# Layer 0's mixture of experts: the residual in SBUF, two zeroed tables of sums, and the fold of layer 1's weights among the expert blocks

## The chip, the core and the metric

The kernel runs on one core of a Trainium2 chip. The metric is device time in microseconds (us) of one execution. Engines are named as the profile names them: PE is TensorE (matmul), PEld its weight load, DVE VectorE, ACT ScalarE, POOL GpSimd, SP SyncE. SP, ACT and POOL can also issue DMA transfers; the indirect ones (gather and scatter by a list of rows) are issued by POOL.

## What is computed

Four layers, each a gated cross-attention and a gated feed-forward, act on x of 4 x 256 tokens with 256 features. The change is in the feed-forward of layer 0, a mixture of 16 experts (hidden width 176) of which every token takes 6, beside one shared expert (hidden width 352):

```python
x = x + tanh(g_ffn[0]) * L0_ffn(layernorm(x), ...)

def L0_ffn(x, ...):
    probs = softmax(x @ gate_w.T)
    _, idx = top_k(probs + gate_b, 6)
    cw = probs at idx, 0 elsewhere                       # (T, 16)
    y = sum over e of cw[:, e] * ((silu(x @ W1[e].T + B1[e]) * (x @ W3[e].T + B3[e])) @ W2[e].T + B2[e])
    z = (silu(x @ ws1.T + bs1) * (x @ ws3.T + bs3)) @ ws2.T + bs2
    return y + z
```

Layer 1's attention needs products of its own weight matrices only (`Wq`, `w_kc_q`, `W_qr`, `W_kr`, `w_kc_kv`, `Wo`), with no token in them. The kernel folds them ahead, inside layer 0's mixture; this is called the fold.

## The kernel before

The program is written with a layer that inserts all waits and that orders each engine's instructions ahead of time by the program's order and an estimate of when operands are ready; so instructions can stand in another order on an engine than in the code. The 1024 tokens are 8 tiles of 128 (`x[t]`, views of one SBUF tensor `stream`). Tiles with one tag share a fixed number of buffers: `xn` six, `t4` six, the weight slots `C` three (`C_SLOTS`), PSUM `mm` four and `wide` two.

**Weights through the slots.** `loads` (L234 to L241) is a list of weight loads in order of use: layer 0's, then layer 1's fold (`L1_qr`, `L1_kv`, `L1_qk0/1`, `L1_wq0/1`, `L1_wo0/1`), layer 1's feed-forward (`L1_w1`, `L1_w2`), then layers 2 and 3. `used(name)` (L253) frees a slot and issues the next load on SP, each as one DMA of up to 1 MB (`whole`, L207).

**`ffn0` (L1391), the mixture.** It normalises x, stores the normal rows to DRAM (`xd`), and makes a generator `routing()` that goes step by step through `chosen` (softmax, top 6) and `placed` (L1061: which tokens fall into which block of 128 rows). The last six steps of `placed` make, for each of the 6 choices and each of the 8 token tiles, two float16 one-hots on VectorE: `h` (L1132, 128x128) and `v` (L1133, 128x63), whose product on TensorE (L1137) adds up the row numbers. L1148 to L1150 make the lists `scatter` and `gather` from them.

Beside the routing runs the shared expert in 14 units: `up(g, f)` (matmuls at L424, Silu L1431, product L1432) and `down(t)` (L1441), whose result `gated_add` (L458) multiplies by the gate and adds to `x[t]`, in one VectorE instruction that reads PSUM. After each unit comes one routing step, and from the third unit on one step of the fold (`fold1`, L783: matmuls at L794, L812, L825 and, in `fold_output`, L581; eleven steps with work). While a fold step is made, `busy` sends its copies from PSUM to ScalarE (`evacuate`, L136).

Then `keep_rows` (L371) writes x to the DRAM table `sums0[0]`. The second table `sums0[1]` was zeroed during layer 0's attention (L353). The class `Experts` (L1180) works through the blocks. 55 blocks (`SURE0`) are always used; those beyond stand under an `If` on the number of blocks, which comes first in the program (L1351). `blocks` (L1358) goes over i:

- `fetch(i + 4)`: POOL gathers 128 rows of `xd` (L1206) into one of the `xn` buffers
- `turn(i)`: two PE transposes (L1218), a DVE copy (L1219), the tokens' weight (L1230), and a load of the expert's offset into a PE register (L1240) from `near`, which DVE copies for eight blocks at once at every eighth block (L1223)
- `turn_hidden(i - 2)`: transposes of the hidden rows (L1280), an ACT copy (L1282)
- `up(i - 1)`: the bias (L1249), the products (L1253), Silu on ACT (L1272), the product on DVE (L1273)
- `down(i - 2)`: products (L1290), a copy into `ring` by DVE or ACT (L1299, L1301), and POOL's scatter that adds the rows to one of the two DRAM tables in turn (L1305)
- `between(i)`: whatever is left of the fold, which is nothing by then.

The last three blocks (`HOT0`) are not scattered. Their results stay in SBUF, DVE makes one-hots `hits` for them (L1323) during the loop, and `add` (L1331) multiplies them on PE (L1339) and adds them to x (L1341). Before that, `collect` (L1477) loads table 0 over x, table 1 into `more`, and adds the two (L1488). Layer 1's attention begins with a layer norm (L382 to L397) and transposes (L409).

Of the kernel before, what the change touches and what calls it, by code (L numbers as in the profile page):

```python
# [30 lines left out]
F32 = mybir.dt.float32  # L31
# [8 lines left out]
P = 128  # L40
# [42 lines left out]
C_SLOTS = 3  # L83
FIXED = 2 * DC + 8 + 2 * E0 + E0 + 8 + 2 * E3 + 4 + NB0 + 8 + 2 * NT + 1 + L + 1 + 2 * len(HS0)
# [4 lines left out]
def tile_flamingo(ctx: ExitStack, tc: tile.TileContext, a: dict, out: bass.AP):  # L89
# [116 lines left out]

    def whole(src, parts=P):  # L207
        def load(w):
            nc.sync.dma_start(out=w[:parts, : src.shape[1]], in_=src)

        return load

    def halves(src, n):
        def load(w):
            nc.sync.dma_start(
                out=w[:, : n * src.shape[1]].rearrange("p (c f) -> p c f", c=n),
                in_=src.rearrange("(c p) f -> p c f", p=P),
            )

        return load  # L220

    def head_attention(layer, quant):
        def load(w):
            nc.sync.dma_start(out=w[:, :1024], in_=a[f"L{layer}_q_out"])
            nc.sync.dma_start(out=w[:DC, 1024:1536], in_=a[f"L{layer}_kv"])
            if quant:
                nc.sync.dma_start(
                    out=w[:, 1536:2048].rearrange("p (c d) -> p c d", c=2),
                    in_=a["L2_weight"].rearrange("(c p) d -> p c d", p=P),
                )  # L230

        return load

    loads = [(f"L0_qk{i}", whole(a["L0_qk"][i])) for i in range(NQ)]  # L234
# [10 lines left out]
    def issue(upto=C_SLOTS):  # L245
        while at[0] < len(loads) and at[0] - at[1] < upto:
            name, load = loads[at[0]]
            w = sb.tile([P, 2048], F32, tag="C", name=f"w_{name}", bufs=C_SLOTS)
            load(w)
            loaded[name] = w  # L250
            at[0] += 1

# [53 lines left out]
    def prepare():  # L306
# [46 lines left out]
        for half in range(2):  # L353
            zeroed(sums0[1][half * TH : (half + 1) * TH], zeros)
# [248 lines left out]
    def streamed(name, cols, n):  # L603

        return [
            lambda i=i: (loaded[f"{name}{i}"][:, :cols], n, lambda: used(f"{name}{i}")) for i in range(2)
        ]
# [175 lines left out]
    def fold1():  # L783


        w_qr = loaded["L1_qr"][:CQH].rearrange("q (s h r) -> q s h r", s=2, h=NH)
        inner = t4([P, NP, DK], "inner")
        for h8 in range(2):
            w_kcT = loaded[f"L1_qk{h8}"][:CQH].rearrange("q (h s k) -> q h s k", h=NP, s=2)
# [16 lines left out]
        w_kr = loaded["L1_kv"][:, NH * DC : NH * DC + NP * DC].rearrange("r (i d) -> r i d", i=NP)  # L806
# [13 lines left out]
        for h8 in range(2):  # L820
            w_q = loaded[f"L1_wq{h8}"].rearrange("k (h d) -> k h d", h=NP)
# [569 lines left out]
    def ffn0(gate):  # L1391
# [17 lines left out]
        def folded():  # L1409
            if ended:  # L1410
                return
# [491 lines left out]
```

## Time and profile before

| | |
|---|---|
| median of 3 runs | 934.46 us (933.23 to 937.22) |
| the profiled execution | 937.0 us, its span 934.9 us |
| granted TensorE clock, mean | 0.963 of full speed |
| PE busy | 850.5 us, 91% of the span |
| DVE, ACT, POOL busy | 515.8, 286.1, 317.9 us |
| shared expert and routing | from about 222 us to 272 us of the span |
| first gather, last gather, last scatter issued at | 268.35, 432.88, 448.20 us |
| last expert matmul of the loop ends | 443.9 us |
| first transpose of layer 1's attention | 463.93 us |

A line of a view in order of time has: start, duration, engine, line of the kernel, operation, out<-in with shapes, how many, and in brackets the idle time of that engine before it with what ended it. A line of the costliest groups has: line, engine, operation, out<-in, shapes, count, then busy time in us and the mean of one in ns, then idle time before it and what ended most of that. Busy time of POOL's indirect DMAs is the time to make the transfer's descriptors, not the transfer.

### The profile page before, as it was taken

The page shows a single profiled execution, that of the slowest core. Times are in us where ns is not written, and L with a number is a line of the kernel's source. Part 1 is how long each engine was busy: PE and PEld are TensorE (multiplying, and loading weights), DVE is VectorE, ACT ScalarE, POOL GpSimd, SP SyncE. Part 2 cuts the span into 40 slices and gives each one's busy share as a digit, 9 for nine tenths or more (in the row PEclk, how much of TensorE's full clock was granted, in tenths as well). Part 3 has the DMA queues.
Part 4 walks back from the last instruction along what each step waited for, and adds up shares of the span by engine and source line. Part 5 has one row for each costly group of instructions (what it writes and reads, how often), then busy time and mean ns, then how long its engine had stood idle before and what let it go on. Part 6 is the DMA issues. An engine that isn't in the chain of part 4 may idle for free.

```text
span 934.9 us, 12575 instructions
## 1 busy us (share of the span) xinstructions
PE 850.5 (91%) x4395; PEld 544.5 (58%) x4395; DVE 515.8 (55%) x1319; ACT 286.1 (31%) x545; POOL 317.9 (34%) x248
## 2 busy tenths in 40 slices
PE   5999998999978999899599978999889899999993
PEld 3544335875746777576446864755555556566662
DVE  3667446755843435333466787968767864222220
ACT  1221103434212332223133428526535531122220
POOL 0445442320027888887102220003202402244321
PEclk8999999999989999999899999989889999999997
DMA  9410218101684554555740000450000012122222
GB/s 343 139 35 6 96 48 270 48 23 28 215 248 82 87 87 80 85 83 80 219 159 1 1 1 1 143 200 1 1 23 1 1 47 64 46 47 46 35 23 63
DMA packets 38481, 74.90 MB, mean 80 GB/s; under 512 B 6225, under 2 KB 26290, under 8 KB 37042
## 3 DMA queue, kind: packets, MB, share of 16 engines
q1 hardware_dynamic: 24050, 53.34, 16.7%
q0 software_dynamic: 14016, 19.94, 13.4%
q8 instruction: 39, 0.64, 0.3%
q10 hardware_dynamic: 352, 0.79, 0.2%
q14 instruction: 24, 0.20, 0.1%
HBM read 58.87 MB, written 16.22 MB: 80 GB/s over the span
## 4 chain that ended last, share of the span: by engine, by line
PE 74%; DVE 9%; DMA 8%; ACT 4%; issue 2%; POOL 2%; SPq 0%; another core or an unknown queue 0%; POOLq 0%; ACTq 0%; DVEq 0%
PE wide L424 14%; PE wide L1264 8%; PE mm L1290 7%; PE wide L1253 6%; PE mm L424 5%; PE mm L659 4%; DMA xs<-xd,big 2%; PE wide L644 2%; PE mm L1665 2%; PE mm L454 2%; PE mm L1649 2%; PE mm L1280 2%; DMA sums<-ring,big 2%; PE wide L944 2%; PE mm L709 2%
## 5 line engine op out<-in xcount | busy, mean ns | idle before, releaser
L440 POOL TENSOR_TENSOR attn<-attn,sm 128x1024 f32<-128x1024 f32 x32 | 60.8, 1901 | 281.9 <-DVE sm L439 228.5
L1273 DVE SCALAR_TENSOR_TENSOR blk<-wide,blk 128x176 f32<-128x176 f32 (+1 forms) x75 | 37.0, 494 | 148.0 <-ACT blk L1272 141.0
L424 PE MATMUL wide<-xT,big 128*128 128x512 f32 (+1 forms) x240 | 111.3, 611 | 0.3 <-ACT xT L140 0.2
L1305 POOL DMA_INDIRECT sums<-ring,big x52 | 82.7, 1590 | 18.7 <-issue 7.8
L686 DVE TENSOR_TENSOR rope<-wide,big 128x512 f32<-128x512 f32 x96 | 59.6, 684 | 50.1 <-PE wide L424 50.1
L1253 PE MATMUL wide<-big,blk 128*128 x220 | 79.2, 478 | 3.3 <-issue 1.6
L1206 POOL DMA_INDIRECT xs<-xd,big x55 | 56.1, 1019 | 67.0 <-PE mm L581 43.1
L424 PEld LDWEIGHTS wide<-xT,big 128*128 128x128 f32 (+1 forms) x240 | 44.1, 192 | 57.1 <-issue 49.8
L1264 PE MATMUL wide<-big,blk 128*128 x160 | 74.3, 606 | 2.6 <-DMA sums<-x 2.2
L1272 ACT ACTIVATE blk<-wide 128x176 f32<-128x176 f32 (+1 forms) x75 | 29.4, 392 | 137.5 <-PE wide L1264 69.0
L1290 PE MATMUL mm<-big,blk 88*128 x220 | 58.2, 385 | 2.8 <-ACT blk L1282 2.1
L659 PE MATMUL mm<-vo,attnT 128*128 128x256 f32 x256 | 58.6, 382 | 1.5 <-ACT attnT L455 1.5
L1290 PEld LDWEIGHTS mm<-big,blk 88*128 88x128 f32 x220 | 42.0, 193 | 19.4 <-ACT blk L1282 3.8
L659 PEld LDWEIGHTS mm<-vo,attnT 128*128 128x128 f32 x256 | 47.4, 190 | 9.0 <-ACT attnT L455 3.2
L1253 PEld LDWEIGHTS wide<-big,blk 128*128 128x128 f32 x220 | 40.6, 197 | 18.6 <-issue 6.1
L455 ACT COPY attnT<-mm 128x512 f32<-128x512 f32 x64 | 34.6, 588 | 53.6 <-PE mm L454 53.2
L1264 PEld LDWEIGHTS wide<-big,blk 128*128 128x128 f32 x160 | 29.3, 194 | 33.3 <-issue 33.3
L438 DVE TENSOR_REDUCE sm<-attn 128x16 f32<-128x1024 f32 x32 | 38.9, 1215 | 16.2 <-ACT attn L432 13.7
L1305 POOL DMA_INDIRECT sums<-ring,scratch x20 | 31.5, 1573 | 41.0 <-ACT ring L1301 17.0
L1206 POOL DMA_INDIRECT xs<-xd,scratch x20 | 19.4, 972 | 73.5 <-PE mm L1218 49.7
L1219 DVE COPY blk<-mm 128x256 f32<-128x256 f32 x75 | 31.4, 419 | 17.0 <-PE mm L1218 14.4
L454 PE MATMUL mm<-ident,attn 128*128 128x128 f32 x256 | 35.1, 282 | 6.2 <-POOL attn L440 6.1
(311 smaller groups left out, 1607.2 us busy)
## 6 DMA issues: line engine op xcount, KB each, us to landing
big<-in_L_w_gate_up SPq DMA_DIRECT2D x8, 1024.0 KB, 8.9
big<-in_L_w SPq DMA_DIRECT2D x3, 1408.0 KB, 8.1
big<-in_L_w_down SPq DMA_DIRECT2D x8, 512.0 KB, 6.1
w_L_qk<-in_L_qk SPq DMA_DIRECT2D x4, 896.0 KB
big<-in_L_w SPq DMA_DIRECT2D x3, 768.0 KB, 7.1
big<-in_L_wo SPq DMA_DIRECT2D x1, 2048.0 KB, 13.0
xd<-xn SPq DMA_DIRECT2D x16, 128.0 KB, 1.8
w_L_wq<-in_L_wq SPq DMA_DIRECT2D x2, 1024.0 KB, 4.8
```

The costliest lines, as they stand in the source:

```text
L424: nc.tensor.matmul(ps, w(c), xT[:, c, :], start=(c == 0), stop=(c == 1))
L438: nc.vector.tensor_reduce(sm, e, AX.X, ALU.add)
L440: nc.gpsimd.tensor_tensor(e, e, sm.unsqueeze(2).to_broadcast([P, groups, n]), ALU.mult)
L454: nc.tensor.transpose(ps[:, i * P : (i + 1) * P], ev[:, pr * P : (pr + 1) * P], ident)
L659: nc.tensor.matmul(ps[:, :D], aT[:, s, :], vo[:, s, :], start=(s == 0), stop=(s == NP - 1))
L686: nc.vector.tensor_tensor(m[:, s, :].rearrange("q (b t) -> q b t", t=S), ps[:, s, :].rearrange("q (b t) -> q b t", t=S), table, ALU.mult,)
L1206: nc.gpsimd.indirect_dma_start(out=xs, out_offset=None, in_=self.xd, in_offset=bass.IndirectOffsetOnAxis(ap=self.gather[:, b : b + 1].bitc ...
L1253: nc.tensor.matmul(ps[:, 0, : 2 * n], st[:, c * P : (c + 1) * P], self.w[:, bass.ds(r + c * 2 * n, 2 * n)], start=False, stop=(c == 1),)
L1264: nc.tensor.matmul(ps[:, k, :n], st[:, c * P : (c + 1) * P], self.w[:, bass.ds(r + (2 * c + k) * n, n)], start=(c == 0), stop=(c == 1),)
L1273: self.weighted = nc.vector.scalar_tensor_tensor(s, lin, self.weight.pop(b), s, ALU.mult, ALU.mult)
L1290: nc.tensor.matmul(ps[:, :D], hT[:k, j * P : (j + 1) * P], self.w[:k, bass.ds(r + j * D, D)], start=(j == 0), stop=(j == self.n - 1),)
L1305: nc.gpsimd.indirect_dma_start(out=self.sums[b % len(self.sums)], out_offset=bass.IndirectOffsetOnAxis(ap=self.scatter[:, b : b + 1].bitca ...
```

## The change

Six things in one diff; the computed result is the same.

1. x stays in SBUF. `keep_rows` is not called for layer 0; both tables are zeroed during layer 0's attention. `collect` loads both tables into four `t4` tiles, table 0 on SP and table 1 on ACT, and returns `last`, which adds the two tables to x on DVE (eight adds where there were four), after the held blocks' `add`.
2. The fold is no longer stepped in the shared expert's units but in `between(i)`, at i = 5, 9, ..., 49: eleven steps with work, a twelfth that ends it. Its copies alternate between ACT and DVE.
3. During the loop (`paced`) weight loads are cut in pieces of 512 columns; one piece is issued after each block, and `ready(name)` issues what is still missing of a tile before its use.
4. The shared expert's result is multiplied by the gate on ACT into an `xn` tile, and added to `x[t]` on POOL.
5. The one-hots `v` of token tiles 3 to 7 are made on POOL (30 of 48).
6. `near` is copied four blocks before its first use, except for block 0.

```diff
     def whole(src, parts=P):
-        def load(w):
-            nc.sync.dma_start(out=w[:parts, : src.shape[1]], in_=src)
-        return load
+        def pieces(w):
+            n = src.shape[1]
+            step = PIECE if paced[0] else n
+            return [move(w[:parts, i : min(i + step, n)], src[:, i : min(i + step, n)]) for i in range(0, n, step)]
+        return pieces
...
     def issue(upto=C_SLOTS):
         while at[0] < len(loads) and at[0] - at[1] < upto:
-            name, load = loads[at[0]]
+            name, pieces = loads[at[0]]
             w = sb.tile([P, 2048], F32, tag="C", name=f"w_{name}", bufs=C_SLOTS)
-            load(w)
+            waiting.extend((name, piece) for piece in pieces(w))
             loaded[name] = w
             at[0] += 1
+        if not paced[0]:
+            forward(len(waiting))
+
+    def forward(n):
+        for _ in range(min(n, len(waiting))):
+            waiting.pop(0)[1]()
+
+    def ready(name):
+        while any(name == of for of, _ in waiting):
+            forward(1)
+        return loaded[name]
...
-        for half in range(2):
-            zeroed(sums0[1][half * TH : (half + 1) * TH], zeros)
+        for sums in sums0:
+            for half in range(2):
+                zeroed(sums[half * TH : (half + 1) * TH], zeros)
...
-                nc.vector.tensor_scalar(
+                engine = nc.vector if t < alone else nc.gpsimd
+                engine.tensor_scalar(
                     v[:, t, :], block16[:, :nb], blk[:, m : m + 1], number[:, t : t + 1], ALU.is_equal, ALU.mult
                 )
...
-            if b < self.sure and b % 8 == 0:
-                n = min(8, self.sure - b)
-                self.near = small([1, 8], "near", 2, I32)
-                behind(nc.vector.tensor_copy(self.near[:, :n], self.offset[0:1, b : b + n]), copied)
+            if b < self.sure:
+                for first in [b] * (b == 0) + [b + 4] * (b % 8 == 4):
+                    n = min(8, self.sure - first)
+                    if n > 0:
+                        self.near[first // 8] = small([1, 8], "near", 2, I32)
+                        behind(nc.vector.tensor_copy(self.near[first // 8][:, :n], self.offset[0:1, first : first + n]), copied)
...
-                collect()
+                last = collect()
                 self.add(self.held)
+                last()
...
-            gated_add(t, ps[:, :D], gate)
+            y = sb.tile([P, D], F32, tag="xn", name="y", bufs=6)
+            nc.scalar.mul(y, ps[:, :D], gate)
+            nc.gpsimd.tensor_tensor(x[t], x[t], y, ALU.add)
...
-            if i >= 2:
-                folded()
...
-        keep_rows(sums0[0], 0)
...
+        fold = fold1()
+        ended = []
+        paced[0] = True
+
         def between(i):
-            folded()
+            if i > 4 and i % 4 == 1 and not ended:
+                try:
+                    next(fold)
+                except StopIteration as end:
+                    ended.append(end.value)
+            forward(1)
...
         def collect():
-            more = [t4([P, TPG, D], "more") for _ in range(NG)]
-            groups = [slice(g * TPG, (g + 1) * TPG) for g in range(NG)]
+            more = []
             for g in range(NG):
-                nc.sync.dma_start(out=stream[:, groups[g], :], in_=tiled(sums0[0], 0)[:, groups[g], :])
-            for g in range(NG):
-                nc.sync.dma_start(out=more[g], in_=tiled(sums0[1], 0)[:, groups[g], :])
-            for t in range(0, NT, 2):
-                two, its = slice(t, t + 2), slice(t % TPG, t % TPG + 2)
-                added.append(
-                    nc.vector.tensor_tensor(stream[:, two, :], stream[:, two, :], more[t // TPG][:, its, :], ALU.add)
-                )
+                for sums, engine in zip(sums0, (nc.sync, nc.scalar)):
+                    m = t4([P, TPG, D], "more")
+                    engine.dma_start(out=m, in_=tiled(sums, 0)[:, g * TPG : (g + 1) * TPG, :])
+                    more.append(m)
+
+            def last():
+                for t in range(0, NT, 2):
+                    two, its = stream[:, t : t + 2, :], slice(t % TPG, t % TPG + 2)
+                    for m in more[t // TPG * 2 :][:2]:
+                        added.append(nc.vector.tensor_tensor(two, two, m[:, its, :], ALU.add))
+            return last
...
         moe.run(SURE0, collect)
+        paced[0] = False
+        forward(len(waiting))
```

`placed` is called with `alone=3` for layer 0 and with its default (all tiles on DVE) for layer 3. `head_attention` cuts its first load in the same pieces.

## The prediction, as put on record

> **What bounds it now.** I read the page first, then busy time by stretch of the span, then each engine's instructions in order of time around layer 0's mixture (222 to 464 us), then the waits. The mixture has three parts: the shared expert with the routing (to 272), the block loop (to 444), and the collecting of the sums (to 464). The first view is busy time by stretch: PE, PEld, DVE, ACT and POOL busy (instructions), granted clock, DMA share, GB/s.
> ```profile
> 230.00:270.00 40.00, 39.73 (x309) 28.06 (x311) 32.34 (x139) 8.39 (x14) 1.34 (x2) 1.00 0.60 192
> ...
> 274.00:278.00 4.00, 1.38 (x6) 0.67 (x6) 1.27 (x7) 0.00 (x0) 1.35 (x2) 0.65 1.00 385
> 278.00:282.00 4.00, 4.00 (x9) 2.30 (x10) 1.12 (x6) 0.32 (x1) 0.00 (x0) 0.50 0.74 218
> ...
> 300.00:350.00 50.00, 48.44 (x233) 35.95 (x232) 20.71 (x84) 15.35 (x44) 40.56 (x32) 1.00 0.55 88
> ```
> In the routing TensorE is full (39.73 of 40) and VectorE nearly so, while GpSimd idles. At the hand-over (274 to 282) TensorE stands, the clock falls to 0.65 and 0.50 and the DMA engines are saturated. In the loop TensorE and GpSimd both look busy; GpSimd's order of time says which is the bound:
> ```profile
> 274.71 0.94 POOL L1206 DMA_INDIRECT xs<-xd,big  x1 [0.30 <-issue]
> 283.46 0.94 POOL L1206 DMA_INDIRECT xs<-xd,big  x1 [7.81 <-PE wide L1253]
> ...
> 293.59 0.99 POOL L1206 DMA_INDIRECT xs<-xd,big  x1 [0.30 <-PE wide L1253]
> 294.88 1.58 POOL L1305 DMA_INDIRECT sums<-ring,big  x1 [0.30 <-ACT blk L1272]
> 296.77 0.99 POOL L1206 DMA_INDIRECT xs<-xd,big  x1 [0.30 <-issue]
> ```
> After a hole of 7.81 us GpSimd runs gather and scatter back to back with 0.30 between: 0.99 + 0.30 + 1.58 + 0.30 = 3.18 us a block. TensorE needs 2.68 (a block's first transpose starts at 402.55, the next at 405.23). So GpSimd's queue bounds the loop; TensorE leads, then from 378 waits for gathers, and has 0.5 us a block to spare. Last, the end in TensorE's order:
> ```profile
> 442.80 1.13 PE L1290 MATMUL mm<-big,blk 88*128 x4 [0.46 <-ACT blk L1282]
> 443.77 10.52 PE L1339 MATMUL mm<-ring,hits 128*128 128x256 f32 x48
> 463.93 2.21 PE L409 MATMUL mm<-ident,xn 128*128 128x128 f32 x8 [9.63 <-DVE xn L397]
> ```
> The held blocks' products (10.5 us) hide behind the last scatters; then TensorE waits 9.63 us for table loads (landed 456.6), adds and layer norm.
>
> **Step 1, the routing.** Fold1's matmuls leave it: 2 x 1.97 (L794) + 2.00 (L812) + 1.89 + 1.97 + 1.97 + 1.98 (L825) + 4 x 1.08 (L581) = 18.1 us of stretches, each overlapping its neighbour by about 0.15; 16.6 net. Its TensorE end falls from 271.9 to 255.3. VectorE then decides:
> ```profile
> L1133 DVE TENSOR_SCALAR big<-fixed,big,fixed 128x63 f16<-128x63 f16 x48 | 14.8, 308 | 0.0
> L1132 DVE TENSOR_SCALAR big<-fixed,big 128x128 f16<-128x128 f16 x48 | 12.3, 258 | 0.0
> L459 DVE SCALAR_TENSOR_TENSOR x<-mm,tg,x 128x256 f32<-128x256 f32 x8 | 3.9, 484 | 7.3 <-PE mm L1441 4.6 <-issue 2.0 <-PE mm L1137 0.7
> ```
> Its one-hots start when L1122 is done (239.5) and end at 264.5, with 7.3 us of waits ahead of the gated adds. From start to start L1132 takes 0.163, L1133 0.205, L459 0.40. After the change 48 x 0.163 + 18 x 0.205 = 11.5 us stay on VectorE, and one L1432 (0.7): 251.7 if nothing holds them. The eight multiplications go to ScalarE (a 128x256 copy from PSUM, L1301, 0.37: 3.0 us, where it is busy 8.4 of 40).
>
> GpSimd gets 30 one-hots and eight adds. No row shows its tensor_scalar. From below: a memset of 128x64, 0.15; from above and far: a gather's issue, 0.99; nearest: its multiply of 128x64 (L440), 0.294, of the same size, so 30 x 0.294 = 8.8. An add of 128x256 lies between its 128x128 (0.40) and 128x512 (1.27): 0.69, eight are 5.5. Does it run beside VectorE? One row bears on it:
> ```profile
> 353.96 1.22 DVE L1323 TENSOR_TENSOR hits<-fixed,at 128x1024 f32<-128x1024 f16 x1
> ```
> ```profile
> 354.05 2.00 POOL L1206 DMA_INDIRECT xs<-xd,big  x1 [0.30 <-DVE at L1320]
> ```
> A gather of 0.99 took 2.00: it ended 0.87 after the VectorE instruction, as if held until that was done. (L440 beside VectorE's work on PSUM stays between 1.896 and 1.904.) So the bounds are: side by side, where TensorE's 255.3 and the last multiplication and add (0.37 + 0.69) end it, first gather at 256.4; or everything in turn, 239.5 + 11.5 + 0.7 + 8.8 + 5.5 + 0.95 (L1148 to L1150) = 267. I take one-hots in turn (SBUF to SBUF on both sides, like L1323) and the adds in the holes that this leaves: 239.5 + 11.5 + 0.7 + 8.8 + 0.95 = **261.5**, against 268.35: **-6.9** (-12.0 to -1.3).
>
> The Trainium skill (SBUF — State Buffer, "Who interferes with whom") speaks against this edit: VectorE's tensor_scalar in a two-port mode and a GpSimd instruction exclude each other for the whole instruction. By that rule the start is 261.5 to 267, without it 256.4. The same section says a tensor_tensor did not hold up descriptor generation; the 2.00 above differs, and the measurement decides.
>
> The new waits: an add on GpSimd waits for ScalarE, and behind it stand the next one-hots, for which TensorE's routing products wait, and at last the first gathers. keep_rows' eight writes (0.32 to 0.70 each on SP) and fold1's loads leave SP's queue.
>
> **Step 2, hand-over and loop.** Before, 175.6 us from the first gather (268.35) to the last expert matmul (443.9). The saturated DMA at 274 was layer 1's and 2's weights and keep_rows; with them gone I let block 0 turn 4 us after the first gather instead of 6.0 (a gather lands some 2.9 after its issue: the chain shows 2.87 at 378.21), and GpSimd's hole shrinks. TensorE idles again, so I keep 4 us for the low clock (L1253 x4 takes 2.68 at 277.98, 1.35 at 284.60). Then 54 steps x 2.68 + 7.8 (436.13 to 443.93) = 152.5, fold1's 16.6 in twelve steps, and 2 for its copies: two of 0.585 to 0.69 in four blocks, half of them now on VectorE, where L1273 to L1280 has about 0.1 to spare. Sum 179.1. GpSimd's own bound: from fetch 6 to the end of fetch 54 it took 150.4; fetch 6 now some 11 after the first gather, plus 10.1 from there to the last matmul: 171.5; up to 5.6 more if three scatters are put sooner in its order (3 x 1.88). So TensorE takes over as the bound, at 3.05 a block against 3.18 while folding: **+3.5**. Its stalls for `near` (0.7 at each eighth block: 299.45 to 302.17 in the chain) were free before and would now cost 4; copying four blocks ahead takes them away, so I count nothing.
>
> **Step 3, the end.** From the last expert matmul to L409: 20.0 before. The held products stay, 10.5 plus 0.1 to 0.3; scatters and table loads now finish beside them. If the program's order on VectorE (all four L1341, then eight table adds) holds, 0.8 + 4 x 0.61 + the layer norm, in all some 7 as from 456.75 to 463.39, follow: 17.9. If table adds and statistics of the first tiles come between the products, as L382 came between L1341s before, nothing follows: 10.6. I take the middle, 14: **-6.0** (-9.4 to -2.1). ScalarE now issues two loads and waits there for table 1; behind it stands only L385, which needs the same sums.
>
> **At nothing.** Zeroing table 0 (two writes of 512 KB, landing in 2.6) falls where slices 3 and 4 of the page show DMA at 1 and 0. The 32 pieces of up to 256 KB take 0.7 us each at the 385 GB/s of 274 to 278, so the loop's DMA share goes from 0.55 to about 0.75; gathers have four blocks of lead, and a scatter lands 4.2 to 4.4 after its start, its table's next coming after 6.4. Without that cover, a scatter landing 2 us later makes GpSimd wait at each block. The pieces wait on SP for free slots; nothing else stands there until the collecting. Layer 1's feed-forward weights are in by block 48, layer 2's by 52. The first scatter no longer waits for keep_rows.
>
> Sum: -6.9 + 3.5 - 6.0 = -9.4, rounded to -9. The profiled execution took 937.0 (span 934.9, 2.1 around it): 928.0. The median of the runs shown is 934.46, 2.5 lower: **925.5**.
>
> **Rivals.** (a) Forecast: 925.5, by itself 919 to 931; chance 0.46. (b) VectorE and GpSimd run side by side and the end closes up: -12.0 + 3.5 - 9.4 = -18: 916.5. For it: L440's steady times. Against it: L1323. 0.24. (c) The gain is spent: everything in turn and the long end, -1.3 + 3.5 - 2.1 = 0: 934.5. The folding then only swaps a full TensorE in the routing for one in the loop, and the change does not do what it says. For it: 3.05 against 3.18 leaves 7 us in all. 0.16. (d) Slower: GpSimd's one-hots are dear. In turn, the start is 239.5 + 13.15 + 30p; with steps 2 and 3 at -2.5 it decides from a start of 270.9, so from p = 0.61 us. At the gather's 0.99 it is 282.4 in turn (+11.5: 946) or 239.5 + 29.7 + 5.5 + 0.95 = 275.7 side by side (+4.8: 939). For it: each GpSimd DMA instruction costs 0.9 or more. Against it: its small arithmetic rows are 0.28 to 0.40. 0.14.
>
> A measurement of this kernel tells about 0.5% from no change, 4.7 us: faster is below 929.8. (a) gives 0.42 to that, (b) 0.24: 0.66. The same: 0.04 of (a) and 0.14 of (c): 0.18. Slower: (d) and 0.02 of (c): 0.16. The range is 914 to 938; it leaves out most of (d), a little beyond (b).
>
> **What would show it.** Right: L1133 on POOL near 0.3; first gather at 256 to 267; block 0 about 4 later with DMA share far under 1; L794 to L581 among the blocks; no 0.6 us hole at every eighth block; L1339 no longer followed by 9.6 us of idle TensorE. Wrong: one-hots on POOL over 0.6; GpSimd waits in the loop for landings of sums; TensorE waits for pieces or fold1's copies of more than 0.5 us per fold step; weights late in attention 1.

## The result and the profile after

| | before | predicted | after |
|---|---|---|---|
| median | 935.37 us (933.23 to 941.77, 8 runs) | 925.5 | 944.19 us (941.29 to 947.87, 8 runs) |
| the profiled execution, its span | 937.0, 934.9 | 928.0 | 943.25, 941.4 |
| granted clock, mean | 0.963 | | 0.954 |
| first gather | 268.35 | 261.5 | 263.21 |
| first scatter issued | 288.46 | | 277.52 |
| last scatter issued | 448.20 | | 444.73 |
| last expert matmul ends | 443.9 | 440.6 | 456.70 |
| first transpose of layer 1's attention | 463.93 | 454.6 | 470.40 |

The ratio after to before is **1.0081** (95% interval 1.0054 to 1.0109): slower, where a gain of 9 us was forecast. From the first attention transpose to the end both spans have 471.0 us left, so the whole loss of 6.5 us lies before it. The table says where: up to the last scatter the changed kernel is ahead, by 10.9 and then 3.5 us; the last expert matmul, which used to come 4 us before the last scatter's issue, comes 12 us after it.

Busy time by stretch of the changed kernel, columns as in the prediction:

```profile
230.00:270.00 40.00, 28.33 (x123) 16.48 (x122) 28.26 (x108) 5.85 (x11) 29.47 (x44) 0.84 0.16 45
...
278.00:282.00 4.00, 4.00 (x22) 3.17 (x22) 2.14 (x8) 1.43 (x4) 3.39 (x3) 1.00 0.50 98
300.00:350.00 50.00, 50.00 (x289) 39.80 (x288) 19.94 (x76) 15.47 (x43) 38.06 (x31) 1.00 0.65 142
434.00:452.00 18.00, 5.85 (x26) 3.96 (x25) 1.70 (x5) 1.86 (x6) 7.80 (x6) 0.80 0.56 106
```

Three lines are as forecast: TensorE is no longer full in the routing (28.33 of 40) and GpSimd is busy there, the hand-over at 278 is smooth, and in the loop TensorE shows no gap. The fourth is not: from 434 to 452 TensorE works 5.85 of 18 us. ScalarE's order of time in that stretch gives the reason (ACTq marks the issue of a transfer):

```profile
436.94 0.32 ACT L1303 ACTIVATE blk<-wide 128x176 f32<-128x176 f32 x1 [1.02 <-PE wide L1284]
450.58 0.34 ACTq L1510 DMA_DIRECT2D more<-sums  x1
450.96 0.37 ACT L1332 COPY ring<-mm 128x256 f32<-128x256 f32 x1 [13.71 <-DMA sums<-ring,big]
...
451.23 0.37 ACT L1313 COPY blk<-mm 89x256 f32<-89x256 f32 x1
```

The issue of table 1's load stands ahead of the copies of the last blocks (L1332, L1313), and waits until the last scatter into table 1 has landed. ScalarE takes its instructions in their order, so the copies, which wait for nothing of the sort, wait 13.71 us with it. TensorE in order of time shows who waits for them:

```profile
438.19 1.35 PE L1284 MATMUL wide<-big,blk 128*128 x4
451.66 2.08 PE L1321 MATMUL mm<-big,blk 88*128 x4 [12.12 <-ACT blk L1313]
...
456.48 11.46 PE L1370 MATMUL mm<-ring,hits 128*128 128x256 f32 x48
470.40 0.41 PE L436 MATMUL mm<-ident,xn 128*128 128x128 f32 x2 [2.46 <-DVE xn L424]
```

After 12.12 us without work the same four products take 2.08 us where they took 1.03 at 436.69 (the granted clock was 0.50 from 451 to 458), and the held products, which should run beside the last scatters, begin 11.8 us after the last one's issue.

The order on ScalarE is not that of the code, in which the loads come behind all blocks. The program's layer orders by an estimate of when operands are ready; the place it chose would fit scatters that land sooner than they do here (argued, not tried).

### The profile page after: what moved, and what is told of

It is laid out like the page before. It is cut to its first block, busy times and chain, and to the rows that moved or that the text cites. A ratio compares the mean times of both kernels' runs of the same rounds, so it can differ in the third digit from the quotient of the medians.

```text
span 941.4 us, 12661 instructions
## 1 busy us (share of the span) xinstructions
PE 853.2 (91%) x4392; PEld 548.0 (58%) x4395; DVE 517.3 (55%) x1291; ACT 286.3 (30%) x547; POOL 340.9 (36%) x286
## 4 chain that ended last, share of the span: by engine, by line
PE 39%; DVE 6%; ACT 3%; issue 1%; POOL 1%; DMA 1%; POOLq 0%; ACTq 0%; DVEq 0%
PE wide L1295 8%; PE mm L451 5%; PE mm L1321 4%; PE wide L451 3%; PE mm L1697 2%; PE mm L1681 2%; PE wide L971 2%; PE mm L481 2%; PE mm L1013 2%; PE mm L1573 1%; PE mm L686 1%; PE wide L671 1%; PE mm L1769 1%; PE mm L436 1%; PE mm L1311 1%; DVE sm L465 1%
## 5 line engine op out<-in xcount | busy, mean ns | idle before, releaser
L1284 PE MATMUL wide<-big,blk 128*128 x220 | 77.4, 474 | 1.4 <-DVE own L1261 1.4
L1295 PE MATMUL wide<-big,blk 128*128 x160 | 73.7, 605 | 2.2 <-DMA sums<-x 2.2
L1321 PE MATMUL mm<-big,blk 88*128 x220 | 59.1, 391 | 12.6 <-ACT blk L1313 12.6
L1321 PEld LDWEIGHTS mm<-big,blk 88*128 88x128 f32 x220 | 42.8, 196 | 28.6 <-ACT blk L1313 13.9
L465 DVE TENSOR_REDUCE sm<-attn 128x16 f32<-128x1024 f32 x32 | 38.9, 1215 | 16.2 <-ACT attn L459 13.7
L1336 POOL DMA_INDIRECT sums<-ring,scratch x20 | 31.5, 1573 | 39.8 <-ACT ring L1332 16.6
```

The source lines that it names most:

```text
L465: nc.vector.tensor_reduce(sm, e, AX.X, ALU.add)
L1284: nc.tensor.matmul(ps[:, 0, : 2 * n], st[:, c * P : (c + 1) * P], self.w[:, bass.ds(r + c * 2 * n, 2 * n)], start=False, stop=(c == 1),)
L1295: nc.tensor.matmul(ps[:, k, :n], st[:, c * P : (c + 1) * P], self.w[:, bass.ds(r + (2 * c + k) * n, n)], start=(c == 0), stop=(c == 1),)
L1321: nc.tensor.matmul(ps[:, :D], hT[:k, j * P : (j + 1) * P], self.w[:k, bass.ds(r + j * D, D)], start=(j == 0), stop=(j == self.n - 1),)
L1336: nc.gpsimd.indirect_dma_start(out=self.sums[b % len(self.sums)], out_offset=bass.IndirectOffsetOnAxis(ap=self.scatter[:, b : b + 1].bitca ...
```

## The experiments

Ratios are to the kernel before, timed on the same chip, with the 95% interval. "Behind the last scatter" is the time from the last scatter's issue to the first attention transpose in the profiled execution: 15.7 us before, 25.7 after.

### Which part holds the end: e1, e5, e6, e14

e1 is the changed kernel with table 1 on SP:

```diff
-                for sums, engine in zip(sums0, (nc.sync, nc.scalar)):
+                for sums, engine in zip(sums0, (nc.sync, nc.sync)):
```

> The changed kernel with one edit: the collecting's loads of table 1 are issued on SP, beside those of table 0, and no longer on ACT. Theory 1 (ACT's queue): in the changed kernel ACT stands 13.7 us (437.3 to 451.0) in front of the load of table 1, which waits for the last scatter, and the last blocks' copies L1313 stand behind it; TensorE waits 12.1 us for them. With the loads on SP this hole goes, the last expert matmul ends near 444 instead of 456.7, and what is late next is the landing of table 1 (450.4, loads landed 455.5): layer 1's first transpose near 460 instead of 470.4, so about 10 us less than the changed kernel, near 934. Theory 2 (the loop itself is what got slower, the hole only stands where the sums would be waited for anyway): at most 3 us less, 941 or more. Theory 3 (GpSimd's dear one-hots are the loss): no change here.

Ratio 1.003 (1.0009 to 1.005); 18.3 behind the last scatter, last expert matmul at 444.84, before the last scatter's issue (448.06) again. The hold is gone, but the first attention transpose comes at 466.37, 4.0 us sooner than as changed, where Theory 1 said about 10: 3 us are missing behind the last scatter, and the last scatter itself is issued 3.3 us later. The median, 941.11, lies just inside Theory 2's band; against its cause speaks that the hold and the late products went with this one edit.

e5 is the kernel before with part 1 of the change alone (residual in SBUF, two zeroed tables, the new `collect` and `last`), and e6 the same with e1's edit.

> The kernel before with part 1 alone: x stays in SBUF, two zeroed tables, the collecting's loads of table 1 on ACT, the adds after the held blocks. Fold, one-hots, shared adds and near as before. Theory 1: the same wait stands in ACT's queue; table 1's last scatter lands at about 452.6, so TensorE waits from about 441 to 453 for copies, the held products come after that: slower than before by 6 to 10 us, 942 to 945. Theory 2 (the loop got slower by the fold among the blocks): nothing of that is here, so the time is that of before or 1 to 3 us less, 932 to 935.

> As e5_part1 with the loads of both tables on SP. Theory 1: no hole, the held blocks' adds leave the path behind the table loads (four L1341 of 0.66) and keep_rows leaves SP and the DMA queues at the hand-over: 2 to 5 us under before, 930 to 933. Theory 2: the same as e5_part1.

e5: 1.0121 (1.0084 to 1.0159), 24.0 behind the last scatter. e6: 1.0016 (0.9993 to 1.0039), 16.8. So the loss sits in part 1, without any of the others, and hangs on the engine of two issues: 7.3 us between e5 and e6, 7.4 between the changed kernel and e1. Both medians missed the figures of Theory 1 upwards: 950.6 against 942 to 945, and 938.99 against 930 to 933. With this end part 1 gains nothing even without the hold.

Is it the engine or the place in its order? e14 leaves the loads on ScalarE and orders them behind its last copy, which is handed to `collect` as `after`:

```diff
+                self.lastcopy = nc.scalar.copy(y, ps[:, :D])
...
+                    if engine is nc.scalar:
+                        behind(ld, after)
```

> The changed kernel with one thing added: ScalarE issues its two loads of table 1 behind its last copy of the expert blocks (L1332), not in front of it; they stay on ScalarE. Theory 1 (in the changed kernel the issue waited in front of three last copies for table 1's last scatter, 13.7 us, and TensorE's last products behind them at half clock; the place in the queue is the cause, not the engine): last expert matmul within 3 us of the last scatter's issue instead of 12 us after it, first attention 1 transpose 16 to 19 us behind the last scatter instead of 25.7, median 936 to 941, as e1 (ratio about 1.000 to 1.004). Rival (the loads are dear on ScalarE wherever they stand, or table 1's loads are late for another reason): 943 to 945, as the changed kernel.

Ratio **0.9984** (0.9967 to 1.0001), against 1.0081 as changed: one order between two instructions is worth about 1%. ScalarE and TensorE of e14 in order of time:

```profile
444.21 0.37 ACT L1332 COPY ring<-mm 128x256 f32<-128x256 f32 x1 [1.22 <-PE mm L1321]
449.96 0.83 ACTq L1510 DMA_DIRECT2D more<-sums  x2
```
```profile
444.01 10.52 PE L1370 MATMUL mm<-ring,hits 128*128 128x256 f32 x48
462.75 0.66 PE L436 MATMUL mm<-ident,xn 128*128 128x128 f32 x2 [8.21 <-DVE xn L424]
```

The issue comes as late (449.96 against 450.58), but behind the copies; the held products start at 444.01, at full clock (1.00 from 434 to 452), before the last scatter is issued (445.23).

### What else the end costs: e9, e12, e13, e15, e19

In e14 TensorE still waits 8.21 us for VectorE, whose order of time in that kernel is:

```profile
454.07 0.69 DVE L1519 TENSOR_TENSOR x<-x,more 128x512 f32<-128x512 f32 x1 [1.95 <-DMA more<-sums]
...
455.47 0.67 DVE L1372 TENSOR_TENSOR x<-mm,x 128x512 f32<-128x512 f32 x1
...
457.98 0.67 DVE L1372 TENSOR_TENSOR x<-mm,x 128x512 f32<-128x512 f32 x1
...
460.88 0.66 DVE L1372 TENSOR_TENSOR x<-mm,x 128x512 f32<-128x512 f32 x1
...
462.20 0.40 DVE L424 TENSOR_SCALAR xn<-x,mv,rstd 128x256 f32<-128x256 f32 x1
```

Three of the four held adds (L1372), whose products had ended with 454.53 at the latest, stand behind a table add that waits for its load; group 1's table adds stand ahead of group 0's layer norm. From the landing (454.07) to the first normalisation (462.20) pass 8.1 us.

e9 is e1 with another order on VectorE: all held adds, group 0's table adds, its layer norm, then group 1's adds (`group(g, after)` makes four table adds behind `after`; `group1` is called after group 0's layer norm):

```diff
-                last()
+                last(self.heldadd)
...
+            def last(after):
+                group(0, after)
+                kept["group1"] = lambda: group(1, kept["normal"])
```

> The changed kernel with all table loads on SyncE (as in e1) and another order on VectorE at the end: all four adds of the held products first, then the two tables' adds of group 0, its layer norm, and only then the adds of group 1. Theory A (in e1 three held adds and group 1's table adds stood between the landing of group 0's sums at 457.7 and its layer norm: 8.7 us, of which only two adds of 0.69, the statistics and the first normalisation, some 4.5 us together, are needed): first attention 1 transpose about 4 us sooner than in e1 with respect to the last scatter (14.3 instead of 18.3), median 936.5 to 938. Rival B (the landing of the loads is late in any case, the order has no weight): within 1 us of e1 (940 to 942).

Ratio 0.9992 (0.9969 to 1.0016), but 17.9 behind the last scatter where 14.3 was expected: the aim was missed, for a reason of the same kind as the first. The median, 936.82, lies in Theory A's band all the same, but by luck: against e1 the last scatter came 2.1 us sooner (445.94 against 448.06), the end hardly. VectorE in e9:

```profile
457.66 0.34 DVE L1751 TENSOR_SCALAR kept<-kept,tg 1x256 f32<-1x256 f32 x1 [6.81 <-DMA kept<-in_L_bias]
457.93 0.67 DVE L1375 TENSOR_TENSOR x<-mm,x 128x512 f32<-128x512 f32 x1
```

A scaling of layer 2's bias, needed much later, now stood ahead of the last held add, and its 1 KB load stood on SP behind the four table loads. e12 and e13 have that wait too, of 3.48 and 1.29 us: 16.4 and 16.8 behind the last scatter.

e12 is e9 with all one-hots on VectorE, e13 e9 with the gated adds on VectorE as well.

> e9 (loads on SyncE, held adds and group 0 first at the end) with all one-hots on VectorE as in e3. Theory A (the end's order and the one-hots' place are independent: e9 came 0.4% under e1, e3 0.3% under e1): ratio about 0.996, median 932.5 to 934.5. Rival B (e3's gain over e1 was chance, the first gathers differ by 0.8 us only): as e9, ratio 0.999 to 1.000.

> e11 with the end's order of e9. Theory A: e11's time less 3 to 4 us, 934 to 938. Rival B (the order of the end is worth nothing once the lists are late): within 1 us of e11.

e12: 1.0003 (0.9983 to 1.0024); e13: 1.001 (0.9986 to 1.0033). Neither differs from e9; e12 missed its Theory A (0.996), and e13 (939.07) is within 1 us of e11 as its Rival B said.

e15 is e14 with the order as meant: three held adds, group 0's table adds, its layer norm, the last held add, group 1's table adds, and the bias scaled behind the layer norm. (`rest` makes the held add of two tiles; `others` is called after group 0's layer norm.)

```diff
+                if t < NT - 2:
+                    made = rest()
+            return made, rest
...
+                def others():
+                    made = rest()
+                    behind(made, kept["normal"])
+                    group(1, made)
...
+        behind(nc.vector.tensor_scalar(bias_2, bias_2, gate[:1], None, ALU.mult), kept["normal"])
```

> e14 (table 1's loads on ScalarE behind its last copy) with VectorE's order at the end mended too: three held adds, the four table adds of group 0, its layer norm, then the last held add and group 1's table adds; the bias of layer 2, whose load stands behind the tables' loads on SyncE, is scaled later (in e12 its wait stood in front of the last held add, 3.5 us). Theory A (the end is now two adds, statistics and one normalisation behind the landing of group 0's second table: 454.07 + 1.4 + 2.1 + 1.3 in e14's profile, 458.9 instead of 462.75): first attention 1 transpose 13 to 14.5 us behind the last scatter, median 3 to 4 us below e14, ratio 0.994 to 0.996. Rival B (the landing itself moves, or what VectorE saves is waited for elsewhere): ratio 0.998, as e14.

Ratio **0.9943** (0.9916 to 0.997), 14.0 behind the last scatter: 3.5 less than e14, as reckoned. VectorE in e15, where between the last landing and the normalised tiles stands only what they need:

```profile
456.28 1.29 DVE L1523 TENSOR_TENSOR x<-x,more 128x512 f32<-128x512 f32 x2 [1.77 <-DMA more<-sums]
457.49 0.75 DVE L409 BATCH_NORM_STATS2 st<-x 128x6 f32<-128x256 f32 x2
...
459.82 1.38 DVE L424 TENSOR_SCALAR xn<-x,mv,rstd 128x256 f32<-128x256 f32 x4
```

e19 gives this end to the kernel before: part 1 alone, loads late on ScalarE, VectorE's order mended.

> The kernel before with the residual kept in SBUF (the two zeroed tables) alone, table 1's loads on ScalarE behind its last copy, and the end's order of e15: what the end's mended form is worth without the fold's move, the GpSimd adds and one-hots. Theory A (e6, the same part with another end, had 1.0016; the mended end takes 3 to 4 us off it, and the other parts are worth some 0.4% of their own): first attention 1 transpose 13 to 14.5 us behind the last scatter, ratio 0.997 to 1.000. Rival B (the whole of e15's gain is the end, the other parts are worth nothing): ratio 0.993 to 0.996.

Ratio 0.9957 (0.9928 to 0.9986), 13.3 behind the last scatter: in Rival B's band. So most of what e15 gains, part 1 with the mended end gives by itself; what the rest of the change adds to e15 (0.0014) is inside the uncertainty.

### The routing: e3, e7, e8, e11

e3 is e1 with all one-hots on VectorE (`alone` 3 becomes `NT`), e7 e1 with 18 instead of 30 on GpSimd (3 becomes 5), e11 e3 with `gated_add` back on VectorE.

> As e1_sp, and all 48 one-hots v on VectorE again; the shared expert's adds stay on GpSimd. The one-hots took 0.57 to 0.64 us on GpSimd, so that its queue of one-hots and adds ran without a gap from 238.7 to 262.1 and set the first gather (263.2). Theory 3: with them on VectorE its chain is 239.3 + 48 x (0.163 + 0.205) + 0.7 + 0.95 = 258.6, the first gather comes near 260, 3 to 4 us sooner, and the time is 3 to 4 us under e1_sp: 930 to 931. Rival (the move pays, as the prediction had it, since VectorE would wait for TensorE again): the first gather at 263 or later, no gain over e1_sp or a loss.

> The changed kernel with all table loads on SyncE (as in e1) and 5 of 8 routing one-hots on VectorE instead of 3, so 18 on GpSimd instead of 30. In e1 a one-hot took 0.57 to 0.64 us on GpSimd and the 30 of them with the 8 shared adds kept it busy without a gap until the lists were done. Theory A (the two engines are badly balanced, and an even split is worth what VectorE alone saves per one-hot, 0.2 us each): 18 x 0.2 = 3.6 us less VectorE work than in e3, and first gather 2.5 to 3.5 us sooner than in e1 (263.5), near 260.5; of this the loop gives back a part, since its end is set by TensorE and GpSimd; median 938 to 940 against 941.1 for e1. Rival B (the two engines hold each other up when both run, so the split makes no difference): first gather within 1 us of 263.5 and the median within 1 us of e1.

> e3 (all table loads on SyncE, all one-hots on VectorE) with the shared part's gated adds back on VectorE too: of the change only the residual's tables and the move of the fold with its load pieces are left. Theory A (the adds on GpSimd bought VectorE some 8 x 0.4 us ahead of the lists): first gather 2 to 3.5 us later than in e3 (264.3), median 938 to 941 against 937.3 for e3. Rival B (the multiplications on ScalarE and the adds on GpSimd bought nothing, because they ended late): first gather within 1 us of e3, median 936 to 938.

| | one-hots on GpSimd | first gather | ratio |
|---|---|---|---|
| e1 | 30 | 263.48 | 1.003 (1.0009 to 1.005) |
| e7 | 18 | 261.01 | 1.0008 (0.9987 to 1.0028) |
| e3 | 0 | 264.28 | 0.9998 (0.9975 to 1.002) |
| e11 | 0, adds on VectorE | 262.79 | 1.0006 (0.9984 to 1.0028) |

e7's first gather came 2.5 us sooner than e1's, at the edge of what its Theory A said. Between 30 and none the lists do not move by a microsecond: with 30 GpSimd ends last, with none VectorE does. In time e3, e7 and e11 cannot be told apart. e3 came nowhere near the 930 to 931 expected, which was reckoned from the 934 expected of e1; its median, 937.26, is the forecast 3 to 4 us under e1's, but not by a sooner first gather. Between e9 and e12, also 30 against none, there is no such difference.

e11's first gather fits neither theory: 1.5 us sooner than e3's. GpSimd's adds are dear to VectorE. In the changed kernel a one-hot on VectorE that meets two of them takes 2.02 us where 0.29 is usual, and ends when they end:

```profile
251.49 2.02 DVE L1161 TENSOR_SCALAR big<-fixed,big,fixed 128x63 f16<-128x63 f16 x1
```
```profile
252.07 1.40 POOL L1469 TENSOR_TENSOR x<-x,y 128x256 f32<-128x256 f32 x2
```

In e3 a VectorE one-hot is drawn out in this way beside each of the seven adds from 243 to 256: it takes 0.43 to 0.80 us and ends 0.04 to 0.05 after the add. That is some 2.9 us of VectorE by an estimate (their 4.93 us less 7 x 0.29), nearly the 8 x 0.40 that VectorE's own adds cost, so the adds' move bought it next to nothing; why e11 is even sooner stays open.

e11 has of the change only part 1, the fold's move, its pieces and `near`; e6 has part 1 alone, with the same loads on SP. At 1.0006 and 1.0016 they do not differ: without the work on GpSimd the fold's move is worth nothing that can be measured.

e8 is e1 with the fold back among the shared part's units, whole loads, as before the change (`folded()` after each unit from the third on).

> The changed kernel with all table loads on SyncE (as in e1), but the fold for attention 1 back among the units of the shared part and then one step behind each block, its loads whole and unpaced, as in the kernel before. Theory A (the fold among the blocks only moves its 16.6 us of TensorE work: what the first gather gains is given back in the loop, where TensorE has 20.0 of 20 us): first gather 3 to 6 us later than in e1, first gather to last scatter 4 to 6 us shorter than the 184.6 us of e1, median within 2 us of e1 (939 to 943). Rival B (the fold's move is a real gain that only the end hid): median 945 or more. Rival C (the move costs, by its load pieces beside the scatters too): median 937 or less.

Ratio 1.01 (1.0075 to 1.0125), against 1.003 for e1: Rival B's band. The first gather came at 270.65, the first scatter at 292.62. GpSimd of e8 at the hand-over, in order of time:

```profile
270.65 1.09 POOL L1235 DMA_INDIRECT xs<-xd,big  x1 [0.43 <-ACT wvo L141]
278.99 0.72 POOL L1482 TENSOR_TENSOR x<-x,y 128x256 f32<-128x256 f32 x1 [7.25 <-remote]
279.86 0.98 POOL L1235 DMA_INDIRECT xs<-xd,big  x1
```

The last gated add stands between the first gather and the second, and holds the second for 8 us. ScalarE had its operand ready at 271.92; what else it waited for the profile only calls remote. With GpSimd's adds the fold's place among the blocks, its loads included, is worth 0.7%; without them (e11 against e6) nothing. So the fold's move mends a cost that comes with the adds' move; that the held gather is this cost is argued, not shown. The loads at the hand-over are an untested rival: the first gather's own rows were awaited until 278.71, while the DMA engines were 0.82 busy (274 to 278). Of Theory A one figure came: from first gather to last scatter e8 took 179.6 us, 5.0 less than e1.

### The loop: e10, e16, e17, e18, e20

The first scatter came 10.9 us sooner than before, the last one 3.5. From first to last scatter it took 159.7 us before, 167.2 as changed, 167.0 in e14. The four kernels with neither fold nor pieces among the blocks took 157.6 to 160.0 (e5, e6, e8, e19), so the two together make the loop longer; in e11 and e6, which differ in them and in `near` alone, it is 167.4 and 159.0. e17 and e18 double one suspect each, on e14: e17 issues every paced load piece twice, to the same place; e18 runs the matmuls of L852 twice (6.9 us of TensorE more), with the same result.

```diff
-            waiting.pop(0)[1]()
+            piece = waiting.pop(0)[1]
+            piece()
+            if paced[0]:
+                piece()
```
```diff
-                for i in range(NP):
+                for i in [*range(NP), *range(NP)]:
```

> e14 with every load piece that is issued among the blocks issued twice, the second to the same place with the same data: the loads' cost in the loop doubled. Theory A (the loop gives back the sooner start because its load pieces slow gathers and scatters): first to last scatter grows by 4 us or more from e14's 167.0, median 940 or more. Rival B (the loads are hidden, what returns the gain is TensorE's fold): first to last scatter within 1.5 us of e14, median within 1 us of e14.

> e14 with the fold's four steps of L852 (1.73 us of TensorE each) run twice with the same result: 6.9 us more of TensorE in the loop. Theory A (TensorE is the bound of the loop, 20.0 of 20 us up to 410): first to last scatter grows by 5 to 7 us from 167.0, median 941 to 944. Rival B (GpSimd's chain is the bound and TensorE has slack): grows by less than 2 us, median within 2 us of e14.

e17: first to last scatter 171.3, 4.3 more; ratio 1.0023 (0.9999 to 1.0047) against e14's 0.9984. e18: 169.3, 2.3 more; ratio 0.9988 (0.9964 to 1.0012). The lengths are of one profile each: with the pieces and the fold single, as in e14, ten kernels took 167.0 to 168.1, and e1 170.1. e17 lies above all of them and is slower in time too, as its Theory A said: the bytes cost. e18's 2.3 us lie inside that spread and its time is e14's, so no cost of 6.9 us more TensorE work is shown; it is nearer to its Rival B, and Theory A's 5 to 7 us are not there. GpSimd's waits from 277 to 446 us (total, times, longest), in e14 and in e17:

```profile
POOL sums L1336 <- DMA sums<-ring,big: 4.2, 3, 1.6
```
```profile
POOL sums L1339 <- DMA sums<-ring,big: 8.7, 7, 2.0
```

With twice the pieces GpSimd waits twice as long for the scatter before to land. But kernels with single pieces wait as long (8.8 us as changed, 9.2 in e12) and are not longer from first to last scatter (167.2 and 168.1), so these waits do not show how the bytes cost time. Of the loop's 7.3 us an estimate from e17 is 4.3 for the pieces; how the rest divides, and what the fold's TensorE work has of it, stays open.

e10 is e9 with e7's split, the first two fold steps beside blocks 0 and 1 and the rest behind every fifth block; e16 is e15 with e7's split; e20 is e16 with the weights among the blocks loaded whole (`step = n`).

> e9 with 5 of 8 one-hots on VectorE as in e7, and with the first two steps of the fold beside the first two blocks, where TensorE waits for gathers, and the others behind every fifth block instead of every fourth. Theory A (the parts add up: end -4, routing -2 to -3 of which the loop keeps a part, loop less crowded): 931 to 935, faster than the kernel before by 0.3 to 0.7%. Rival B (the loop's end is set by GpSimd's gathers and scatters whatever starts earlier, so only the end counts): 936.5 to 938, as e9.

> e15 with 5 of 8 one-hots on VectorE as in e7. Theory A (the lists come 2.5 us sooner, as in e7, and the loop keeps them): ratio 0.991 to 0.994. Rival B (TensorE and GpSimd set the loop's end whatever starts it): as e15 within 1 us.

> e16 with the fold's weights loaded whole, 1 MB at one step, and not in pieces of 256 KB, one behind each block. Theory A (e17 showed 4 us more in the loop for twice the bytes; whole loads bring as many bytes in bursts, in which gathers and scatters wait longer): first to last scatter 2 us or more above e16's 167.4, ratio 0.994 to 0.997. Rival B (only the bytes count): first to last scatter within 1.5 us, ratio within 0.002 of e16.

| | first gather | first, last scatter | behind the last scatter | ratio |
|---|---|---|---|---|
| e10 | 261.04 | 280.54, 446.79 | 16.4 | 1.0011 (0.9985 to 1.0038) |
| e15 | 263.71 | 278.73, 446.42 | 14.0 | 0.9943 (0.9916 to 0.997) |
| e16 | 260.94 | 275.58, 443.01 | 14.9 | 0.9915 (0.9879 to 0.9951) |
| e20 | 260.94 | 275.91, 444.20 | 14.0 | 0.9904 (0.9879 to 0.9928) |

e10 was a miss: with fold steps beside the first blocks the first scatter came 4.6 us later than e7's 275.96, and nothing was gained. e16 and e20 beat both kernels: 929.18 us for e20 against 937.99 for the kernel before. Pieces or whole loads make no difference that was measured; it is the bytes that count. e16 is not shown to beat e15 in time (the intervals overlap), though its last scatter is 3.4 us sooner. Against e19, which has the mended end alone, e20's interval just ends where that one begins (0.9928): the rest of the change with e7's split is worth about half a percent, at the edge of what is measured here.

## Why the prediction was wrong, point by point

**The step that failed** is in step 3: "ScalarE now issues two loads and waits there for table 1; behind it stands only L385, which needs the same sums." The wait was foreseen, what stands behind it was taken from the code's order, and the order on the engine is not the code's, as the section on the kernel says itself. Behind it stood four copies and a Silu of the last blocks, and behind these TensorE's last products: 13.71 us of ScalarE, 12.12 of TensorE, 7.3 to 7.4 us of the end. No rival had it: (d), the slower one, laid the loss on the one-hots. The Trainium skill has the rule at work (PSUM — Partial Sum Buffer, "Engine vs sequencer instructions": the queues of ScalarE, VectorE and GpSimd are strictly first in, first out); the 13.71 us agree with it.

**The end's other assumption** fell too. Step 3 took 14 us from the last expert matmul, as a middle between 10.6 with interleaved adds and 17.9 without. After the change it is 13.7, a coincidence: the matmul was so late that both tables had landed. Without the hold it was 18.6 in e14 and 21.5 in e1, beyond the upper bound of 17.9, since the first group's sums land only as the held products end (454.07 against 454.53 in e14, 457.70 against 455.21 in e1), and then the interleaving called good is what costs (8.1 us from the landing to the first normalisation, 3.5 in e15).

**Step 1** was right in size by two errors. The GpSimd one-hot took 0.57 to 0.64 us, not 0.294; and it did not go in turn with VectorE, while the adds, which were to fill holes, did. Busy time by stretch of the changed kernel, GpSimd's one-hots beside VectorE and alone:

```profile
238.70:248.20 9.50, 8.17 (x48) 5.37 (x47) 9.50 (x46) 2.10 (x4) 9.50 (x15) 1.00 0.40 119
257.20:260.05 2.85, 2.65 (x12) 1.77 (x11) 0.00 (x0) 0.27 (x1) 2.85 (x7) 0.50 0.00 0
```

Fifteen took 9.54 us beside a VectorE busy all the time (0.636), five took 2.86 with VectorE idle (0.572): a ninth more, not one after the other. In turn the lists would have been done at 239.5 + 11.5 + 0.7 + 30 x 0.62 + 0.95 = 271.3; the first gather was at 263.21 against 261.5 forecast. Rival (d)'s point of decision, 0.61 us, was reached, but it holds only in turn. The Trainium skill's rule that was weighed (SBUF — State Buffer, "Who interferes with whom": a two-port tensor_scalar of VectorE and a GpSimd instruction exclude each other) is not seen in these rows as a whole-instruction block; whether VectorE was in that mode, the profile does not tell. Beside GpSimd's adds a block of this kind is seen: the one-hot of 2.02 us shown under the routing ended only when both adds had.

**Step 2** was near: 179.1 us from the first gather to the last expert matmul were forecast, 180.1 were measured in e14, where no hold falsifies it (193.5 as changed). The cause given, TensorE as the bound with 16.6 us, is not borne out: e18 had 6.9 us more TensorE work in the loop and e14's time, and its last expert matmul came 180.9 us after the first gather, 0.8 later than e14's. And e17 shows that the pieces, put at nothing because "gathers have four blocks of lead", cost about 4 us. The condition named there ("a scatter landing 2 us later makes GpSimd wait at each block") is met in part: GpSimd's waits for landings of sums from 277 to 446 were 2.6 us before, 4.2 in e14 and 8.8 as changed, but at 3 to 6 scatters and not at each block.

Taken together: in e14, without the hold, the three terms of the sum miss by 2.6 (first gather 264.08), 1.0 (180.1) and 4.6 us (18.6), together the 8.2 between the 454.6 forecast and 462.75; the hold adds another 7.7. With the hold away the change is level with the kernel before (0.9984, interval to 1.0001), which is the time of rival (c), but not its way there: the one-hots did not go in turn. The gain of 4.3 us at the first gather and 10.2 at the first scatter is 3.0 at the last scatter, by the fold and pieces in the loop, and 1.2 at the first transpose, by VectorE's order.

Open stay what the add of e8 waited for, and how the loop's 7.3 us divide; e17 gives a slope for the pieces, not a share.

## What to carry to other kernels

A transfer that waits for something late holds everything behind it on the engine that issues it; before moving an issue onto a compute engine, look in the engine's order as built, not in the code, for what stands behind it, and tie it behind the last instruction that does not need it. The same goes for a small operation on VectorE or GpSimd that waits where others could go on: three such places (L1510 on ScalarE, L1751 on VectorE, L1482 on GpSimd) stood 13.7, 2.9 to 6.8 (e9, e10, e12) and 7.3 us here. Work that is moved out of a full stretch into a loop is only won if the loop has room for its instructions and for its bytes: 10.2 us at the first scatter were 3.0 at the last one here.

## What the runs showed of the hardware that was not expected

- A GpSimd tensor_scalar with two operands per partition (128x63, float16) took 0.57 us alone and 0.64 beside VectorE, twice its 128x64 multiplication (0.294); on VectorE the same takes 0.31.
- A GpSimd add (128x256, float32, both operands in SBUF, 0.72 us) holds a VectorE tensor_scalar beside it until it ends: 2.02 us instead of 0.29 beside two adds as changed, 0.43 to 0.80 beside one in e3. Beside GpSimd's one-hots VectorE's kept their 0.29 (the median of 18 as changed).
- The prediction's row of a gather held by L1323, VectorE's 128x1024 tensor_tensor, is no single case. Each gather or scatter begun beside that instruction (two before, two as changed, two in e14; L1354 in these) took 1.78 to 2.54 us instead of 0.99 or 1.58, and ended 0.86 (gathers) or 1.44 to 1.46 us (scatters) after it.
- After 12 us of waiting TensorE's four products of L1321 took 2.08 us instead of 1.03, and the 48 held products behind them 11.46 instead of 10.52; the granted clock was 0.50 from 451 to 458 and 1.00 from 460 on.
- TensorE can show 20.00 busy of 20 us and still absorb work: with 6.9 us more in the loop e18 had e14's time (0.9988 and 0.9984).
